# Hub blocks of the second attention layer moved into the drain, the gap and the ramp between two layers

## The chip, the cores and the metric

The kernel runs on one core of a Trainium2 chip. The metric is the device time of one execution in microseconds; times given are the median of several executions. The profile comes from one further execution with the hardware profiler on.

## What is computed

The input is a batch of 8 graphs with the same 2048 nodes and 64 features per node, and one adjacency matrix of 2048 x 2048 zeros and ones. Two layers of graph attention are followed by layer normalisations:

```python
def _gat_layer(h, mask, b):
    scores = jnp.einsum('...nd,...md->...nm', h, h)
    scores = jnp.where(mask, scores, NEG)
    attn = jax.nn.softmax(scores, axis=-1)
    return jnp.einsum('...nm,...md->...nd', attn, h) + b

mask = graph + jnp.eye(N, dtype=graph.dtype) > 0
h = jnp.einsum('bnc,hdc->bhnd', x, Wh)              # 4 heads
out_h = _gat_layer(h, mask[None, None], bh[None, :, None, :])
cat = jnp.transpose(out_h, (0, 2, 1, 3)).reshape(B, N, H * D)
z = jax.nn.leaky_relu(cat, negative_slope=0.2)
h2 = jnp.einsum('bnk,dk->bnd', z, Wo)
out2 = _gat_layer(h2, mask[None], bo)               # 1 head
z2 = jax.nn.leaky_relu(out2, negative_slope=0.2)
out = layernorm(z2) * gamma + beta
result = layernorm(x + out)
```

The adjacency is sparse: node k is linked with a probability that falls with its number, so the first nodes have many neighbours and the later ones few.

## The kernel before

**Tiling.** The first 56 nodes (`HUB`) are "hub" nodes and attend to everything. The other 1992 are put into 166 sets of 12 nodes (`NS`, `SET`). For each set the kernel makes a list of at most 128 nodes that some member of the set is linked to; the attention of the 12 members is then computed densely over the 128 rows of that list, with a mask. The rows are fetched with an indirect DMA, issued by GpSimd (`gather`, one per set and layer: 332 in all). A row has the features of all 8 batches, 2080 bytes. `table1` holds the rows for layer 1, `table2` the rows that layer 1 leaves for layer 2, and `table3` the terms x + beta of the last normalisation; all three lie in DRAM.

**Order of the work.** The order of instructions on each engine is the order in which the program writes them; nothing is moved by a planner. So the source is a software pipeline written out by hand, and each engine (TensorE, VectorE, ScalarE, GpSimd) and each DMA queue (SP, ScalarE, GpSimd) works through its own list in that order, waiting where an operand or a buffer isn't ready.

**Stage 0** (about the first 150 us) reads the adjacency, makes the lists for the first 60 sets (the others follow within layer 1), and does the hub nodes of layer 1.

**Layer 1** is a loop `for i in range(-4, NG + 3)` over 83 groups of two sets (`NG`). Iteration i has, for different groups: `scores` (L821), `weigh` (the mask, VectorE, L826), `project` (L531) and `leaky` into `z` (L518), a copy of the transposed rows (`xTg`, L1030), `lift` (exp, L833), `values` (L846), `invert` (reciprocal L853 and product `osb` L854), the gathers of group i + 5, `leak` (L523), `second_maps` (L880) and `second_rows` (L890), `columns` (L806), `keep_own` (L885) and `keep_rows` (L894, and the stores of `rowt` to `table2`, L897), `keep_columns` (the copy `y`, L812), and the transposes of the gathered rows (`turn`, L512) and of the values (L863, copied to `otb`, L870). PSUM is divided in four tiles of two banks with the tags T (transposed rows), S (scores), C (`cat`: projections, maps, rows, columns) and O (values), one buffer each. The iterations i = 83 to 85 are the drain: the last groups pass through the later steps.

**The gap.** Then the pools of stage 0 and layer 1 are closed and those of layer 2 opened (`late`, `psum2`). VectorE clears the buffers of layer 2 (`ownb` L1107, `bd` L1111, `esh` L1113, `es2` L1114 and L1115) and makes the mask `linked` (L1117). The first 24 gathers from `table2` are issued, and four loads of hub rows (L1267).

**Layer 2** is a loop `for u in range(-4, NU + 7)` over 42 groups of four sets (`NU`); u = -4 to -1 is the ramp. Iteration u has `scores2` of u + 2 (L1133, exp at L1136), `values2` of u (L1165), the four gathers of u + 6, `spread_own` (L1124), `turn_scores` (L1144) and `keep_scores` (L1152) of u + 1, and `turn2` of u + 4 (transposes L512, copies `xTg` L1320). The gathered rows have 24 buffers, six groups. The hub nodes attend to all nodes in 18 blocks (17 of ten sets, and the hub itself); `hub_at` says in which iterations they are done: u = -4 to -1 and then every second one from 2 to 28. A block has a load of rows by SP (`hub_block`), `hub_scores2` (L1277), `hub_lift2` (VectorE L1285, exp at L1288) and, two iterations later, `hub_values2` (L1299), which adds into `oh2`.

**Norms.** After each second group the sums of eight sets are normalised (`norm`, lines L1186 to L1222), in eight steps spread over eight iterations: division, leak, mean, centring, sum of squares, root (`roots`, on ScalarE, L1239 and L1240), then gamma, the row of `table3`, and a second normalisation; `store` (L1248) writes eight pieces of 24 KB to the output, issued by SP. Only the last norm issues half of its pieces from ScalarE.

At the end the kernel reads a flag that says whether the lists were long enough; if they weren't, `general_kernel` would compute everything again. With these inputs it doesn't run.

## Time and profile before

| | us |
|---|---|
| median of 3 runs (lowest, highest) | 877.46 (876.76, 881.76) |
| profiled execution | 880.76 |
| its span | 878.9 |
| busy: TensorE, its weight loads, VectorE, ScalarE, GpSimd | 753.0, 661.2, 610.1, 514.4, 469.2 |
| layer 1's last values (L846) begin | 590.42 |
| first gather of layer 2 begins | 605.49 |
| last gather of layer 2 begins | 822.80 |
| the last group of `values2` (L1165) begins | 846.38 |
| VectorE's last instruction ends | 869.43 |

Times within the kernel are counted from the start of the span. The profile names engines PE (TensorE's matmuls), PEld (its weight loads), DVE (VectorE), ACT (ScalarE), POOL (GpSimd) and SP (the SyncE queue, which only issues DMAs here); a q behind a name is the engine's instruction queue, where DMAs are issued. L512 is line 512 of the kernel before. A group is named by line, engine, operation and "written tile <- read tiles". "x16" counts instructions. In a timeline, the bracket gives the idle time before an instruction and what ended it, as inferred from semaphores. The chain of waits is followed back from the last instruction, at each step to what released it; there the times of matmuls are those between their ends. All times of pieces come from the one profiled execution.

### The profile page before, as it was taken

What the parts mean: (1) busy time and instruction counts of PE and PEld (TensorE: products, weight loads), DVE (VectorE), ACT (ScalarE), POOL (GpSimd) and SP (SyncE); (2) the same over time, 40 slices, a digit from 0 to 9 for tenths busy, and PEclk for the clock granted to TensorE, in tenths of its full rate; (3) what the DMA queues carried; (4) which work ended last, traced back from release to release, by engine and by line L of the source; (5) the groups of instructions that cost most, each with busy time, mean ns of one, the idle gap of its engine ahead of it and who ended that gap; (6) DMA issues with size and microseconds to landing.
All of it is one profiled execution on the core that took longest, in us unless ns stands there. A gap on an engine that the chain in (4) does not pass through costs nothing.

```text
span 878.9 us, 42066 instructions
## 1 busy us (share of the span) xinstructions
PE 753.0 (86%) x18437; PEld 661.2 (75%) x18437; DVE 610.1 (69%) x1369; ACT 514.4 (59%) x961; POOL 469.2 (53%) x612
## 2 busy tenths in 40 slices
PE   1896777889999999999999999992999999998730
PEld 1664456778788999988999999971899999988720
DVE  3356983568888788877555555553258999998994
ACT  2342333556556667666766667651678888886821
POOL 5654141457444555655666666503777777777300
PEclk9998998999999999999999999995999999999965
DMA  8787451355434445655566665514888888888611
GB/s 167 238 218 213 129 146 48 83 142 160 109 100 118 112 125 159 162 169 153 160 168 173 160 166 162 134 28 114 246 266 253 275 275 267 266 252 242 172 46 35
DMA packets 81794, 145.22 MB, mean 165 GB/s; under 512 B 30146, under 2 KB 46466, under 8 KB 81602
## 3 DMA queue, kind: packets, MB, share of 16 engines
q0 software_dynamic: 26720, 88.55, 36.4%
q1 hardware_dynamic: 37842, 49.65, 18.7%
q10 hardware_dynamic: 17040, 4.25, 2.6%
q8 instruction: 147, 2.41, 1.1%
q14 instruction: 45, 0.37, 0.1%
HBM read 123.91 MB, written 18.48 MB: 162 GB/s over the span
## 4 chain that ended last, share of the span: by engine, by line
PE 63%; DVE 15%; DMA 7%; ACT 5%; issue 4%; SPq 3%; POOL 2%; DVEq 0%; ACTq 0%; POOLq 0%
PE t L512 11%; PE s L821 10%; PE o L846 10%; PE cat L806 6%; PE o L863 4%; PE cat L531 4%; PE cat L880 3%; PE s L1133 3%; PE o L1165 3%; PE cat L890 2%; DMA raw<-in_adj_dram 2%; SPq L1248 2%; PE sh L1277 2%; PE e L1144 2%; DMA g<-table,index 1%
## 5 line engine op out<-in xcount | busy, mean ns | idle before, releaser
L792 POOL DMA_INDIRECT g<-table,index x332 | 334.9, 1009 | 236.1 <-PE o L846 140.2
L512 PE MATMUL t<-ident,g 128*128 128x128 f32 x1328 | 182.3, 276 | 15.6 <-DMA g<-table,index 12.7
L512 PEld LDWEIGHTS t<-ident,g 128*128 128x128 f32 x1328 | 154.8, 142 | 20.0 <-issue 14.0
L826 DVE TENSOR_TENSOR e<-s,mask 128x768 f32<-128x768 f32 x83 | 79.4, 956 | 87.4 <-PE s L821 85.4
L518 ACT ACTIVATE z<-cat,bhp 128x192 f32<-128x192 f32 x166 | 60.8, 418 | 85.0 <-PE cat L531 85.0
L846 PE MATMUL o<-g,e 128*64 128x65 f32 x2656 | 97.5, 227 | 0.0
L821 PEld LDWEIGHTS s<-y,xTg 64*64 64x64 f32 x5312 | 85.2, 134 | 13.9 <-issue 13.7
L821 PE MATMUL s<-y,xTg 64*64 64x48 f32 x5312 | 95.5, 220 | 0.0
L846 PEld LDWEIGHTS o<-g,e 128*64 128x64 f32 x2656 | 85.8, 140 | 9.8
L1320 ACT COPY xTg<-t 128x1024 f32<-128x1024 f32 x83 | 80.3, 1017 | 18.1 <-PE t L512 17.3
L1030 ACT COPY xTg<-t 128x1024 f32<-128x1024 f32 x83 | 84.0, 1012 | 2.0 <-PE t L512 2.0
L833 ACT ACTIVATE e<-e,shifts 128x768 f32<-128x768 f32 x83 | 79.2, 955 | 2.1 <-DVE e L826 1.7
L812 ACT COPY y<-cat 128x384 f32<-128x384 f32 (+1 forms) x80 | 40.7, 508 | 64.0 <-PE o L863 40.1
L597 ACT ACTIVATE e<-e,shifts 128x896 f32<-128x896 f32 x32 | 33.4, 1042 | 73.0 <-DVE e L594 52.1
L680 POOL TENSOR_SCALAR a<-raw 120x1024 bf16<-120x1024 int32 (+1 forms) x34 | 38.2, 1125 | 65.1 <-DMA raw<-in_adj_dram 38.4
L806 PE MATMUL cat<-xo,gram 128*128 128x192 f32 (+1 forms) x320 | 65.6, 328 | 0.0
L853 DVE RECIPROCAL rall<-o 64x8 f32<-64x8 f32 x166 | 34.0, 205 | 42.0 <-PE o L846 40.7
L854 DVE TENSOR_TENSOR osb<-o,rall 128x512 f32<-128x512 f32 x83 | 57.4, 692 | 2.9
L1165 PE MATMUL o<-g,es 128*32 128x65 f32 x2656 | 49.1, 226 | 5.9 <-DVE y_s L1188 4.5
L806 PEld LDWEIGHTS cat<-xo,gram 128*128 128x128 f32 x320 | 53.7, 203 | 0.3 <-issue 0.2
L1165 PEld LDWEIGHTS o<-g,es 128*32 128x32 f32 x2656 | 46.1, 113 | 7.0 <-issue 4.9
L1133 PE MATMUL s<-xTg,bd 128*32 128x128 f32 x1328 | 45.4, 277 | 6.2 <-ACT bd L1124 3.5
(177 smaller groups left out, 1369.3 us busy)
## 6 DMA issues: line engine op xcount, KB each, us to landing
raw<-in_adj_dram SPq DMA_DIRECT2D x32, 480.0 KB
table<-xb SPq DMA_DIRECT2D x22, 256.0 KB
xr_s<-table SPq DMA_DIRECT2D x21, 256.0 KB
g<-table,index POOLq DMA_INDIRECT x332
table<-x SPq DMA_DIRECT2D x16, 260.0 KB
x<-in_x_dram ACTq DMA_DIRECT2D x32, 128.0 KB
table<-rowt SPq DMA_DIRECT2D x166, 24.4 KB
xb<-in_x_dram SPq DMA_DIRECT2D x164, 24.0 KB
```

The source lines that it names most:

```text
L512: nc.tensor.transpose(tp[:, q * P:(q + 1) * P], rows[:, q, 1:1 + P], ident)
L518: nc.scalar.activation(z[:, hp], cat[:, :, hp * n:(hp + 1) * n], AF.Identity, bias=bhp[:, hp:hp + 1], scale=1.0)
L792: nc.gpsimd.indirect_dma_start(out=t.rearrange("n q c -> n (q c)"), out_offset=None, in_=table, in_offset=bass.IndirectOffsetOnAxis(ap=ind ...
L806: nc.tensor.matmul(cat[:, k, 2 * GM:2 * GM + n], gram[:, g % 2 * 2 + k, :], held["x", g // 2][:, :n], start=True, stop=True)
L821: nc.tensor.matmul(sp[half(r), p, (q * 2 + j) * M:(q * 2 + j + 1) * M], xt[half(p), j, q, half(r)], y[half(p), (j * Q + q) * M:(j * Q + q ...
L826: nc.vector.tensor_tensor(e[:, :16 * M].rearrange("p (a q n) -> p a q n", a=2, q=Q), sp[:, :, :8 * M].rearrange("p a (q n) -> p a q n", q= ...
L833: nc.scalar.activation(e[:, :16 * M], e[:, :16 * M], AF.Exp, bias=shifts[:, 0:1], scale=1.0)
L846: nc.tensor.matmul(op[half(p), j, o0:o0 + K1], e[:, c0:c0 + 64], rw[j][:, q, sums(p)], start=True, stop=True)
L1030: nc.scalar.copy(t, held.pop(("tp", i + 2)))
L1133: nc.tensor.matmul(sp[q * 32:(q + 1) * 32, k, :], bd[u % 3][:, k, q, :], xt[:, s % 2, q, :], start=True, stop=True, tile_position=(0, q * 32))
L1165: nc.tensor.matmul(op[t * 32:(t + 1) * 32, f, k * W2 + p:k * W2 + p + K1], e[:, 2 * q + p, k, :], rw[:, q, sums(p)], start=(a == 0 and k = ...
L1320: nc.scalar.copy(t, tp)
```

## The change

1. *Shared buffers.* A list `share` of six buffers in the pool that lives through the kernel replaces buffers of stage 0 (`wnat`, `wos`, `number`, `yh`, `keys`, `cand`, `best`) and later serves layer 2 (`ownb`, `bd`, `es2`, `esh`). `linked` takes a part of `maskh` that is no longer needed.
2. *Early clearing.* Eleven jobs (clearing `ownb` and copying into it, five clearings of `bd` and `es2`, ends, `linked`, three `spread_own`) are done one at a time in the odd iterations 61 to 81 of layer 1.
3. *Hub steps.* `hub_step(k)` does scores and lift of block k and the values of block k - 1. Steps 0 to 5 run in iterations 80 to 85 of layer 1, steps 6 to 10 in the gap, 11 to 14 in the ramp and 15 to 18 in u = 0 to 3. The order of blocks begins with the hub itself. The rows of the first ten blocks are loaded in iterations 78 to 82 into buffers of layer 1's gathered rows, the next four in the gap. Scores and sums of the hub use the two banks of a PSUM tile `both`, which also takes the place of layer 1's T, of layer 2's scores and of `oh2`.
4. *Drain.* Iteration 84 uses the tag S for `cat` instead of C, and the last two groups issue one of their two stores to `table2` from ScalarE.
5. *Last norms.* The last four set norms are done in three steps over three iterations instead of eight; in three of them the products with gamma and the sums with the row of `table3` go to GpSimd. The hub's norm starts at u = 4. The last norm's eight stores are issued from SP, ScalarE and GpSimd in turn.

The core of the diff:

```diff
+    share = [const.tile([P, n], F32, name=f"share{k}") for k, n in enumerate([HALFN, HALFN, HALFN, 512, 512, 2 * 456])]
...
-            nc.sync.dma_start(out=dst[2 * g + j], in_=r[j * 48:(j + 1) * 48])
+            (nc.scalar if j and g >= NG - 2 else nc.sync).dma_start(out=dst[2 * g + j], in_=r[j * 48:(j + 1) * 48])
...
+    both = psumk.tile([P, 2, 512], F32, name="both")
...
-        return psum1.tile([P, 2, 512], F32, tag=tag, name=name)
+        return both if tag == "T" else psum1.tile([P, 2, 512], F32, tag=tag, name=name)
...
+    def clear_own():
+        nc.vector.memset(ownb, 0.0)
+        for p in range(2):
+            nc.vector.tensor_copy(ownb[half(p), :, p, :], ownh[half(p)].rearrange("c t (k n) -> c (t k) n", k=2))
+    def clear_ends():
+        for k in range(2):
+            nc.vector.memset(esh[k][:, Q * 2 * HUB:], 1.0)
+        nc.vector.memset(es2[0][:, :, :, 24:], 1.0)
+    def link():
+        nc.vector.tensor_scalar(linked, mask.rearrange("p s (k h) -> p s k h", h=H)[:, :, :, 0], 0.0, None, OP.is_equal)
...
+    hub_order = [NHB] + list(range(NHB))
+    oh2 = both[:, 1, :]
...
+    def hub_step(k, sp):
+        if k <= NHB:
+            hub_scores2(k, sp)
+            hub_lift2(k)
+        if 0 < k <= NHB + 1:
+            hub_values2(k - 1)
+    ahead_of_second = ([clear_own] + [lambda t=t: nc.vector.memset(t, 0.0) for t in bd + es2] + [clear_ends, link] +
+                       [lambda u=u: spread_own(u) for u in range(3)])
...
-        cat = one(f"cat{i}", "C")
+        cat = one(f"cat{i}", "C") if i <= NG else None
+        if i < NG:
+            ph, pr = cat[:, 0, 384:384 + GM], cat[:GM, 1, 384:512]
+        else:
+            cat = one(f"cat{i}", "S" if i == NG + 1 else "C")
+            ph, pr = cat[:, 0, :GM], cat[:GM, 1, :P]
...
+        if NG - LOOK <= i < NG:
+            for j in range(2):
+                k = 2 * (i - NG + LOOK) + j
+                hub_block(k, rows_tile(f"gh{k}"))
...
+        if i >= 60 and i % 2 and ahead_of_second:
+            ahead_of_second.pop(0)()
         if 0 <= (i - 30) // 2 <= NV:
             (add_beta if i % 2 else load_own)((i - 30) // 2)
         if 0 <= i - 1 < NG:
             leak(held["z", i - 1])
...
+        if i >= NG - 3:
+            hub_step(i - NG + 3, both[:, 0, :])
+    for k in range(6, 11):
+        hub_step(k, both[:, 0, :])
...
+    xts = [late.tile([P, 2, 512], F32, name=f"xts{k}", bufs=1) for k in range(6)]
+    hrows = [late.tile([P, Q, PW], F32, name=f"hrows{k}", bufs=1) for k in range(4)]
+    for k in range(4):
+        hub_block(10 + k, hrows[k])
     for u in range(6):
         for s in sets[u]:
             gather(table2, s, 2, rows2)
...
-        at = [v + 2, v + 6]
+        quick = 2 * NV - 7 <= v < 2 * NV and nb == 8
+        at = [v + 1, v + 2] if quick else [v + 2, v + 6]
...
         def again():
             scale(0)
-            nc.vector.tensor_tensor(y, y, row(gam), OP.mult)
-            nc.vector.tensor_tensor(y, y, xr[:, :nb], OP.add)
+            eng = nc.gpsimd if quick and v < 2 * NV - 1 else nc.vector
+            eng.tensor_tensor(y, y, row(gam), OP.mult)
+            eng.tensor_tensor(y, y, xr[:, :nb], OP.add)
...
+        if quick:
+            return [([], [first, act, mean(0), centre(0)]), ([var(0)], [again, mean(1), centre(1)]), ([var(1)], [end])]
...
-                    (nc.scalar if v == NV - 1 and a else nc.sync).dma_start(out=dst, in_=y[p0:p0 + SET].rearrange("p (f w) c -> p f (w c)", f=2)[:, :, :w * D])
+                    queue = nc.sync if v < NV - 1 else (nc.sync, nc.scalar, nc.gpsimd)[(2 * t + a) % 3]
+                    queue.dma_start(out=dst, in_=y[p0:p0 + SET].rearrange("p (f w) c -> p f (w c)", f=2)[:, :, :w * D])
...
-        if u - 2 in hub_at:
-            b = hub_at[u - 2]
-            hub_values2(b, b == 0, b == NHB)
...
+        k = u + 15
+        if k <= NHB + 1:
+            hub_step(k, bank2(f"sh{k}", "T", 2)[:, 0, :] if k <= NHB else None)
+            if 10 <= k - 1 and k + 3 <= NHB:
+                hub_block(k + 3, hrows[(k - 1 - 10) % 4])
+        if u == 4:
+            spread(u, norm_hub(u, oh2))
```

## The prediction, written before the changed kernel was run

> **What bounds the kernel now.** I read the busy table by slices first (TensorE at 9 tenths almost everywhere, so the ends of the stages matter), then windows over each stage, then the chain of waits inside the second layer, then the timeline of the gap, of one late iteration of layer 1 and of the end. The windows give, per stage: span, busy PE, PEld, DVE, ACT, POOL, granted clock, DMA share.
>
> ```profile
> 558.50:578.50 20.00, 20.00 (x557) 18.15 (x553) 11.74 (x30) 13.66 (x29) 7.40 (x11) 1.00 0.38 95
> 590.00:600.00 10.00, 6.84 (x96) 5.04 (x96) 3.39 (x11) 2.00 (x6) 0.80 (x3) 0.70 0.06 14
> 700.00:720.00 20.00, 19.77 (x508) 18.34 (x507) 18.31 (x34) 16.19 (x30) 15.26 (x16) 1.00 0.89 276
> 820.00:840.00 20.00, 15.47 (x468) 13.74 (x456) 19.45 (x36) 14.65 (x29) 2.98 (x3) 1.00 0.44 125
> ```
>
> The end of layer 1's loop is pure TensorE (20.00 of 20). The drain (590 to 600) is half idle at a reduced clock. Layer 2 has TensorE at 19.77, but VectorE at 18.31 and DMA at 0.89 stand close behind. After 820 VectorE is the bound. The chain of waits through one pair of layer-2 iterations (start, us, what):
>
> ```profile
> 708.75 1.02 ACT xTg L1320
> 709.78 0.04 issue
> 709.82 1.09 PE sh L1277 x8
> ...
> 713.46 1.75 PE t L512 x16
> ...
> 717.15 0.62 PE oh L1299 x16
> 717.77 0.59 PE e L1144 x4
> 718.36 0.89 PE t L512 x8
> ```
>
> The pair lasts 719.27 - 708.75 = 10.52 us. The hub block costs 0.62 (oh) and, because its scores need a transposing bank, 0.89 + 1.06 + 1.09 where the other iteration has only 1.75: 1.29 more. So 1.91 us per block; without it TensorE needs 8.6 us per pair. But GpSimd's gathers (a pair has 8) have a pace of their own, seen where no buffer holds them:
>
> ```profile
> 606.76 0.95 POOL L792 DMA_INDIRECT g<-table,index  x1 [0.30 <-issue]
> 608.01 0.95 POOL L792 DMA_INDIRECT g<-table,index  x1 [0.30 <-issue]
> ...
> 610.29 1.20 DVE L1117 TENSOR_SCALAR linked<-mask 128x1992 uint8<-128x1992 uint8 x1
> 610.51 1.79 POOL L792 DMA_INDIRECT g<-table,index  x1 [0.30 <-issue]
> ```
>
> One every 1.25 us: 10.0 us per pair. **The floor under layer 2 is therefore the gather queue, 0.5 us below the present pair, not TensorE's 8.6.** The third view is one late iteration of layer 1:
>
> ```profile
> 559.56 0.55 DVE L523 SCALAR_TENSOR_TENSOR z<-z 128x384 f32<-128x384 f32 x1
> 560.19 0.28 DVE L894 TENSOR_TENSOR rowt<-cat,bob 96x128 f32<-96x128 f32 x1
> 560.56 0.51 ACT L812 COPY y<-cat 128x384 f32<-128x384 f32 x1 [0.66 <-PE o L863]
> 560.95 0.54 ACT L870 COPY otb<-o 128x192 f32<-128x192 f32 x2
> 561.79 0.38 PEld L531 LDWEIGHTS cat<-otb,whT 64*64 64x64 f32 x16
> ```
>
> ScalarE's y copy starts 0.09 us after VectorE's rowt in every iteration looked at; otb ends at 561.49 and TensorE's projection begins at 561.79. What delays rowt has about 0.28 us of slack before TensorE stops.
>
> **What the skill says.** "DMA: Bandwidth & Descriptors", section SWDGE vs HWDGE vs iDMA: descriptors of a GpSimd DMA are built by GpSimd's cores in software. The 0.95 us per gather agrees. "SBUF — State Buffer", Who interferes with whom: VectorE and GpSimd share a port pair, and some VectorE forms shut out GpSimd's descriptor writing. The 1.79 us gather beside the 1.20 us linked instruction agrees. "PSUM — Partial Sum Buffer", PSUM bank collisions raise a hardware error: accesses of one bank by two engines have to be kept apart. The 0.09 us agrees with an order kept between VectorE and ScalarE on cat. "TensorE: Matmul & The Clock Gate", Part 1: an idle window takes the clock to half. The 32 values matmuls that take 1.15 us in the loop take 1.88 at 590.42.
>
> **The change part by part.**
>
> 1. *Clearing in the loop.* Eleven jobs go into odd iterations 61 to 81, on VectorE between osb and leak, so ahead of rowt. Their durations are in the gap's timeline: ownb memset and two copies 1.03, three bd memsets 1.57 together, two es memsets 0.91 each plus 0.1 between, ends about 0.45, linked 1.20: 6.2 us in eight VectorE jobs. Less 8 x 0.28 slack: **+3.8 us** on a saturated TensorE (bounds: 0 if y didn't wait for rowt, 5). The three spreads (two copies, 0.70) fit ScalarE's 0.66 us of idle before y: 0. In the gap all of this but the 0.43 ownb memset was hidden beside gathers in flight, so little comes back there.
>
> 2. *Hub blocks in the drain.* Steps 0 to 5 follow the value transposes of iterations 80 to 85. Each has scores (1.03), VectorE lift 0.62, ScalarE exp 0.66, values 0.62. Iteration 80 is saturated: +1.03. From 81 on, values 0.62 join; some of it fills the 0.67 us waits for otb at 589.93 and 595.03, and the clock stays up (0.73 back on the values at 590.42). Followed in order: values 82 end 593.3 instead of 592.3, projection 82 starts 596.6 instead of 595.03, second maps 82 600.6 instead of 597.95, last rowt 603.3 instead of 600.40. The S bank for iteration 84 is in this already: maps 82 no longer wait for rowt 80. The two last stores are issued from SP and ScalarE side by side (0.58 each, now in a row, the last at 601.43) and land 2.04 later: 606.3 instead of 604.1. **+2.2 us** (0 to 4). Ten hub loads of 244 KB take the place of layer-1 gathers on an idle DMA (share 0.05); SP issues each in 0.77 and in those five iterations has 2 x 0.77 + 2 x 0.6 = 2.7 of 4.8 us: 0. First gather of layer 2, in before's clock: 605.5 + 3.8 + 2.2 = 611.5. GpSimd's 0.9 us of queued waits after the last landing stay.
>
> 3. *Gap and ramp.* Steps 6 to 10 run on TensorE at about 1.7 us each while the gathers fly; the first set was usable 5.6 us after its issue. Four hub loads stand ahead of the gathers as four did before: even. Steps 11 to 14 answer to the four blocks that the ramp had; 15 to 18 run in iterations 0 to 3.
>
> 4. *Layer 2.* First to last gather now takes 822.80 - 605.49 = 217.3 us for 165 intervals; at 1.25 it is 206.3. Iterations 0 to 3 with a hub step need about 4.3 + 1.9 = 6.2 us against 5.0. The 24 buffers give set group 6 at 30 us after the first gather; TensorE frees group 0 about 27.5 us after it. After four such iterations it is 1.1 us late, and that remains. 1 us for stray waits: 208.4. VectorE: 19.3 busy of two pairs now, 9.65 per pair, less lift 0.62 = 9.0: under 10.0. **-8.9 us** (bounds -11 and 0, the last if VectorE takes over). The hub's own norm moves to iterations 4 to 11, where the set norms still build up: 0.
>
> 5. *Last norms.* From the gap after iteration 35 VectorE is the bound. Two of 13 instructions in each of three norms go to GpSimd: 0.73 x 2 saved, but the mean stands directly behind them in VectorE's queue and waits for both; at 1.28 each (GpSimd's add of bet, same shape) that is about 2.75: +1.3 net x 3 = +3.9. Gone are the remains of the hub norm (0.8) and some idle. VectorE's work from iteration 36 to its end sums to 47 us against 44.3. In exchange TensorE, ahead of the gathers rather than behind, ends values 35 some 4 us before the last group's gathers are issued (0.9 before now). Sum **-0.8 us** (-5 to +3).
>
> 6. *Stores.* After VectorE's last instruction (869.43) SP still has eight stores of norm 19 and four of norm 20 to issue, until 874.95 (5.5 us). Norm 19 now ends 10 us earlier; norm 20's eight go out on three queues, about 1.6 us on SP and 2 on GpSimd, whose landing is slower. **-3.2 us** (-1 to -4).
>
> Sum: +3.8 + 2.2 - 8.9 - 0.8 - 3.2 = -6.9. The profiled execution took 880.76 us (span 878.9 and 1.9 around it), so 873.9; the median of the runs is 877.46, 3.3 under the profiled one, so I forecast **870.6 us**.
>
> **Rivals.**
> - *The clearing is free and the quick norms pay.* If rowt's delay is absorbed (-3.8) and GpSimd's two steps overlap other VectorE jobs (-3.9): 863. For it: the y copy's named releaser is PE o, not rowt, in most iterations. Against: the same 0.09 us everywhere, also where PE o had ended 0.26 earlier.
> - *The gathers wait for the hub steps.* If the memory of the gathered rows is shared with that of the hub rows in the closing pool, the first gather comes only after step 10: 603.3 + 3.8 + 6 x 1.7 + 0.6 = 617.9, and the 1.3 us of waits and issue give 619.2, 7.7 later: 878.3. For it: the page's first gather waits for something of VectorE's after the landing. Against: the tiles opened ahead of the rows look sized to keep them on older memory.
> - *Slower: VectorE takes TensorE's place in layer 2.* Decides from 5.26 us per iteration without hub work. Then layer 2 gives nothing (-8.9 lost) and the end stays behind VectorE by its 47 us (+3): 870.6 + 8.9 + 3 = 882.5. For it: 18.31 of 20 us busy, 19.45 after 820. Against: there, without hub blocks, iterations of 4.96 to 4.99 us were reached.
>
> **How the numbers follow.** Forecast case 0.50, free clearing 0.27, waiting gathers 0.12, VectorE 0.11. A measurement of this kernel can hardly tell less than 1% (8.8 us) from no change; the bounds are 868.7 and 886.2. Of the forecast's 0.50, with parts 1 to 6 varying, 0.14 lies under 868.7; with most of the second case faster makes 0.40. Slower than 886.2: the upper part of the last case and the forecast's extremes, 0.09. Range 862 to 882: below it a part of the second case, above it half of the last.
>
> **What would show it.** Right: odd layer-1 iterations from 61 on at 5.2 to 5.9 us, with TensorE waiting for otb; first layer-2 gather near 611; its gathers at 1.25 us without a break after iteration 4; layer-2 TensorE with idle ended by gather landings; VectorE idle of 2 to 3 us beside GpSimd in the last three set norms; SP silent 2 us after VectorE ends. Wrong: odd iterations still 5.0; gathers held up by TensorE or VectorE at 5.2 us or more per iteration; the first gather after the hub steps.

## The result and the profile after

The changed kernel takes **913.6 us** (median of 4, 911.01 to 917.09) against 878.0 for the kernel before: ratio 1.0385, 95% interval 1.0348 to 1.0422. I had forecast 870.6 with a range to 882. The profiled execution has a span of 914.2 us, 35.3 more than 878.9. Cut at the same events in both profiles, the 35.3 us lie here:

| stretch | before | after | difference | my sum |
|---|---|---|---|---|
| start to first weigh of layer 1 | 153.4 | 157.7 | +4.3 | 0 |
| first to last weigh | 432.7 | 438.0 | +5.3 | +4.8 |
| last weigh to last rowt | 14.4 | 18.5 | +4.1 | +1.9 |
| last rowt to first gather of layer 2 | 5.1 | 16.2 | **+11.1** | -0.7 |
| first to last gather | 217.3 | 225.8 | **+8.5** | -8.9 |
| last gather to VectorE's last instruction | 46.6 | 52.0 | **+5.4** | -0.8 |
| from there to the end of the span | 9.5 | 6.1 | -3.4 | -3.2 |

(The +1.03 for the first hub scores, which I had in the sum of the drain, falls into the second row; the third row's +1.9 and the fourth's -0.7 are 603.3 for 600.40 and 2.2 in all, less that 1.03.)

The windows of the changed kernel over the end of the layer-1 loop, the drain, the stream of layer 2 and its tail (span, busy PE, PEld, DVE, ACT, POOL, granted clock, DMA share, GB/s):

```profile
568.00:588.00 20.00, 19.36 (x547) 17.52 (x546) 12.02 (x29) 13.67 (x30) 6.78 (x10) 1.00 0.42 112
600.00:610.00 10.00, 6.92 (x134) 5.77 (x134) 4.31 (x12) 3.34 (x8) 0.54 (x2) 1.00 0.31 90
725.00:745.00 20.00, 17.96 (x468) 16.34 (x466) 18.50 (x34) 16.73 (x30) 15.73 (x15) 1.00 0.84 239
856.00:876.00 20.00, 12.05 (x292) 10.71 (x285) 14.36 (x24) 10.19 (x24) 3.63 (x4) 0.83 0.28 76
```

As forecast, the drain's clock stays at 1.00 and TensorE is less busy in layer 2 (17.96 instead of 19.77 of 20). But GpSimd is no faster for it, and in the tail VectorE, which should have been the bound, is busy for only 14.36 of 20 us. The gap of the kernel before, from its last rowt to its first gather (start, us, engine, line, idle before and who ended it):

```profile
600.40 0.29 DVE L894 TENSOR_TENSOR rowt<-cat,bob 96x128 f32<-96x128 f32 x1 [0.61 <-PE cat L890]
605.05 0.43 DVE L1107 MEMSET ownb<- 128x448 f32 x1 [4.36 <-DMA table<-rowt]
605.49 0.96 POOL L792 DMA_INDIRECT g<-table,index  x1 [5.56 <-DVE ownb L1107]
605.51 0.57 DVE L1109 COPY ownb<-ownh 64x224 f32<-64x224 f32 x2
```

The same stretch of the changed kernel:

```profile
614.09 0.29 DVE L895 TENSOR_TENSOR rowt<-cat,bob 96x128 f32<-96x128 f32 x1 [1.07 <-DMA table<-rowt]
...
620.08 0.62 DVE L1074 TENSOR_TENSOR share<-both,maskt 120x448 f32<-120x448 f32 x1 [1.92 <-PE both L1065]
620.80 0.69 PE L1088 MATMUL both<-gh,share 120*64 120x65 f32 x16 [0.83 <-issue]
621.42 1.09 PE L1065 MATMUL both<-share,own 128*120 128x112 f32 x8
622.62 0.62 DVE L1074 TENSOR_TENSOR share<-both,maskt 120x448 f32<-120x448 f32 x1 [1.92 <-PE both L1065]
...
628.77 0.69 PE L1088 MATMUL both<-gh,share 120*64 120x65 f32 x16 [1.19 <-issue]
629.60 3.21 SPq L1054 DMA_DIRECT2D hrows<-table  x4
630.29 0.97 POOL L793 DMA_INDIRECT g<-table,index  x1 [18.07 <-PE both L1088]
```

Before, the first gather comes 5.1 us after the last rowt, once the table's last store has landed. Here the last rowt is at 614.09, yet the first gather starts at 630.29, right behind the values of hub step 10 (628.77), which it names as releaser. And a step takes 2.54 us (620.08 to 622.62), not 1.7: scores, lift and values follow one another, with TensorE idle for 0.83 us ahead of each values. The end of the last norm, where the stores now stand on three queues:

```profile
907.41 0.69 DVE L1299 TENSOR_TENSOR y_s<-y_s,var_True 128x512 f32<-128x512 f32 x1 [0.61 <-ACT var_True L1328]
908.13 1.35 SPq L1337 DMA_DIRECT2D out_dram<-y_s  x3
908.14 1.24 ACTq L1337 DMA_DIRECT2D out_dram<-y_s  x3
908.40 1.28 POOL L1337 DMA_DIRECT2D out_dram<-y_s  x2 [16.43 <-DVE y_s L1299]
```

All are issued within 1.6 us of VectorE's end. This step is as forecast.

One thing is needed to read the runs below: in three of their five sets the kernel before itself took 1,041 to 1,048 us (median), and in every kernel profiled there layer 2's gathers took 297 to 324 us from first to last, with GpSimd waiting for row buffers; from these sets ("slowed transfers") I read the gap, layer 1's loop, the length of single gathers and the tail, and differences of whole times only where I say so.

### The profile page after: what moved, and what is told of

The parts are those of the page before. It is cut to its first block, busy times and chain, and to the rows that moved or that the text cites. A ratio compares the mean times of both kernels' runs of the same rounds, so it can differ in the third digit from the quotient of the medians.

```text
span 914.2 us, 42292 instructions
## 1 busy us (share of the span) xinstructions
PE 765.4 (84%) x18437; PEld 666.5 (73%) x18437; DVE 609.6 (67%) x1363; ACT 519.2 (57%) x969; POOL 485.5 (53%) x620
## 4 chain that ended last, share of the span: by engine, by line
PE 58%; DVE 16%; DMA 10%; ACT 6%; issue 5%; POOL 3%; SPq 2%; ACTq 0%; DVEq 0%; POOLq 0%
PE s L822 9%; PE o L847 9%; PE both L513 8%; PE cat L807 5%; DMA g<-table,index 4%; PE cat L532 4%; PE o L864 3%; DMA raw<-in_adj_dram 3%; PE cat L881 3%; PE t L513 2%; PE cat L891 2%; PE both L1216 2%; DMA table<-x 2%; DVE st_s L1279 2%; PE oh L609 1%
## 5 line engine op out<-in xcount | busy, mean ns | idle before, releaser
L793 POOL DMA_INDIRECT g<-table,index x332 | 342.5, 1032 | 252.8 <-PE o L847 139.2
L513 PE MATMUL both<-ident,g 128*128 128x128 f32 x664 | 100.7, 275 | 2.7 <-DVE share L709 2.5
L513 PE MATMUL t<-ident,g 128*128 128x128 f32 x664 | 87.8, 282 | 17.0 <-DMA g<-table,index 14.6
L1369 ACT COPY xts<-t 128x1024 f32<-128x1024 f32 x83 | 81.1, 1016 | 30.2 <-PE t L513 21.6
L513 PEld LDWEIGHTS t<-ident,g 128*128 128x128 f32 x664 | 76.1, 145 | 22.6 <-DMA g<-table,index 12.8
L1123 ACT COPY xTg<-both 128x1024 f32<-128x1024 f32 x83 | 84.0, 1012 | 1.7 <-PE both L513 1.7
L513 PEld LDWEIGHTS both<-ident,g 128*128 128x128 f32 x664 | 80.1, 142 | 5.8 <-DVE share L709 3.1
L1286 ACT ACTIVATE sq_s<-y_s 128x512 f32<-128x512 f32 x42 | 26.4, 629 | 47.9 <-DVE y_s L1284 47.8
```

The source lines that it names most:

```text
L513: nc.tensor.transpose(tp[:, q * P:(q + 1) * P], rows[:, q, 1:1 + P], ident)
L793: nc.gpsimd.indirect_dma_start(out=t.rearrange("n q c -> n (q c)"), out_offset=None, in_=table, in_offset=bass.IndirectOffsetOnAxis(ap=ind ...
L1123: nc.scalar.copy(t, held.pop(("tp", i + 2)))
L1369: nc.scalar.copy(t, tp)
```

## The experiments

A set is a group of runs made together on one chip. Whole times are compared within a set, beside the runs of the kernel before that it shares; pieces of time come from one profile of each run, and where they are compared across sets the text says so.

### What holds the gathers in the gap

First run (the changed kernel with steps 6 to 9 out of the gap; its hub norm, moved to u = 9, shares a variance buffer with a set norm, which leaves output rows of both wrong):

```diff
...
-                hub_block(k, rows_tile(f"gh{k}"))
+                if k < 6:
+                    hub_block(k, rows_tile(f"gh{k}"))
...
-    for k in range(6, 11):
-        hub_step(k, both[:, 0, :])
+    hub_values2(5)
...
-        hub_block(10 + k, hrows[k])
+        hub_block(6 + k, hrows[k])
...
-        k = u + 15
+        k = u + 10
...
-        if u == 4:
+        if u == 9:
```

> The changed kernel with hub steps 6 to 9 taken out of the gap: only blocks 0 to 5 use the gathered rows' buffers of layer 1, blocks 6 to 9 load into the late hub rows and are worked off in the first iterations of layer 2, four iterations later everything. Theory 'memory': the gathers waited because their rows lie on the memory that hub blocks 0 to 9 used, so with the last such reader (block 5) at the end of the drain the first gather comes about 5 us after the last rowt, near 619.5 instead of 630.3, and the kernel takes 8 to 11 us less than the changed kernel, about 903 to 906. Rival 'order': the gathers wait for something else of the gap (the loads' queue, the table's last stores with the clock), then the first gather stays within 3 us of 630 and the time stays at 910 to 916. If the stream of layer 2 pays for the four steps moved into it (0.6 of GpSimd's row buffers held longer, VectorE 0.62 per step), the gain is 5 to 8.

Second run (the steps of the gap get other banks for their scores):

```diff
     for k in range(6, 11):
-        hub_step(k, both[:, 0, :])
+        hub_step(k, one(f"shs{k}", "SCO"[k % 3])[:, 0, :])
```

> The changed kernel with the scores of hub steps 6 to 10 in the three score, column and value banks that the drain has left free, instead of one bank of the pair whose other bank holds the hub sums. Theory 'pair': values k-1 wait for lift k because both banks belong to one pair, so the wait of 0.83 us per step goes and a step takes about 1.7 us: the first gather comes 4 us earlier (near 626) and the kernel takes 3 to 4.5 us less than the changed one. Rival 'weights': the wait comes from the two halves of the hub weights lying in one buffer; then the steps stay at 2.5 us and the time does not move.

Measured in a set with slowed transfers: 1,035.4 and 1,028.3 us; the kernel before 1,045.6. Last rowt to first gather is 3.8 us in the first run and 11.35 in the second; in the seven profiles with the gap of the changed kernel it is 16.2 to 19.3. In these nine and in the two profiles of the combined run below, the first gather starts 0.84 or 0.85 us after the end of the last values that read the layer-1 row buffers, wherever the edit puts them. (In the second run its bracket names VectorE's lift, which had ended 0.38 us before; in the changed kernel that distance is 1.62.) So the first gather follows the last reader of these buffers: "memory" is shown, "order" falls. Neither run has the changed kernel in its set, so the 8 to 11 us and the 3 to 4.5 us expected of the whole time are not tested. In the timeline of the second run the steps look so:

```profile
644.77 0.62 DVE L1074 TENSOR_TENSOR share<-shs,maskt 120x448 f32<-120x448 f32 x1 [1.01 <-PE shs L1065]
645.21 1.09 PE L1065 MATMUL shs<-share,own 128*120 128x112 f32 x8
646.23 0.69 PE L1088 MATMUL both<-gh,share 120*64 120x65 f32 x16
646.41 0.62 DVE L1074 TENSOR_TENSOR share<-shs,maskt 120x448 f32<-120x448 f32 x1 [1.01 <-PE shs L1065]
...
651.04 0.96 POOL L793 DMA_INDIRECT g<-table,index  x1 [13.22 <-DVE share L1074]
```

1.64 us per step (644.77 to 646.41), and TensorE goes from scores to values without a pause. So "pair" holds: as long as the scores lay in one bank of `both` and the hub sums in the other, values waited for VectorE's lift of the next block. The two halves of the hub weights still lie in one buffer here, so "weights" falls.

### What sets the pace of layer 2

The kernel before without the hub blocks of its steady state, three times (the hub rows of the output are incomplete):

```diff
-    hub_at = {u: b for b, u in enumerate([-4, -3, -2, -1] + list(range(2, 2 * NHB, 2))[:NHB - 3])}
+    hub_at = {u: b for b, u in enumerate([-4, -3, -2, -1])}
...
```

> The kernel before with hub blocks 4 to 17 left out of the second layer (loads, scores, lift and values; the hub rows of the output are then incomplete), the hub's norm at its old place. It prices what the change takes out of the steady state of layer 2. My prediction's theory: the gathers then run at 1.25 us, first to last gather 206 to 209 us instead of 217.3, the kernel at about 869. Rival 'stretch': GpSimd was the bound already, [...]so the blocks cost nearly nothing there: 214 to 217 us, and the kernel stays within 4 us of the kernel before.

> The kernel before with hub blocks 4 to 17 left out of the second layer, as in the run of that kind above, whose transfers were slow. My prediction's theory: gathers at 1.25 us, first to last gather 206 to 209 us instead of 217.3, the kernel about 9 us below the kernel before. Rival 'stretch': GpSimd was the bound already, held up beside VectorE's two-input instructions, and the stream takes 213 to 217 us, the kernel within 4 us of the kernel before.

> Once more the kernel before with hub blocks 4 to 17 left out of layer 2 (incomplete hub rows), beside a kernel before whose transfers are not slowed, if this set has one. My prediction's theory: 206 to 209 us from first to last gather instead of 217.3. Rival 'stretch': 213 to 217 us, as the gathers' own durations summed to 10 us over 0.95 each in the kernel before and fell to 0.95 each once the norms were left out.

The first two fell into sets with slowed transfers (998.6 and 999.6 us beside 1,045.6 and 1,048.1). The third did not: **886.5 us against 880.3**, ratio 1.0072 (1.0047 to 1.0096), and its first to last gather takes 219.2 us, no less than the 217.3 with the hub blocks. Fourteen blocks at 1.9 us of TensorE each bring nothing. That it is even 0.7% slower I can't explain; its profiled execution, the fastest of 16, has the span of the kernel before. In both kernels GpSimd never waits longer than 0.31 us between two gathers of this stretch: it is saturated. A piece of the kernel before:

```profile
705.35 0.69 DVE L1197 TENSOR_REDUCE st_s<-y_s 128x8 f32<-128x512 f32 x1
705.54 0.94 POOL L792 DMA_INDIRECT g<-table,index  x1 [0.30 <-issue]
706.55 0.69 DVE L1202 SCALAR_TENSOR_TENSOR y_s<-st_s,y_s 128x512 f32<-128x512 f32 x1
706.79 1.27 POOL L792 DMA_INDIRECT g<-table,index  x1 [0.30 <-PE o L1165]
```

And of the kernel without the hub blocks:

```profile
703.61 0.68 DVE L1202 SCALAR_TENSOR_TENSOR y_s<-st_s,y_s 128x512 f32<-128x512 f32 x1
703.76 1.35 POOL L792 DMA_INDIRECT g<-table,index  x1 [0.30 <-issue]
705.42 0.94 POOL L792 DMA_INDIRECT g<-table,index  x1 [0.31 <-issue]
706.67 0.95 POOL L792 DMA_INDIRECT g<-table,index  x1 [0.30 <-PE t L512]
```

Some gathers take 1.27 or 1.35 us instead of 0.95. Next, also without the hub blocks, the first 17 set norms are cut:

```diff
+        if i < 17:
+            return [([], [first]), ([lambda: store(y)], [])]
         return [([], [first, act, mean(0)]), ([centre(0)], []), ([var(0)], []), ([], [again, mean(1)]), ([centre(1)], []),
...
```

> The same, and of the first 17 set norms of layer 2 only the division and the store are kept, with all loads and stores (the rest of these norms is left out, so their output rows are not normalised). Theory 'stretch': without VectorE's two-input instructions the gathers take 0.95 us and 0.30 between them, 206 to 209 us from first to last. Rival 'transfers': the DMA engines, at 0.89 before, set the pace, and the stream stays at 213 to 217 us.

> The kernel before without hub blocks 4 to 17 in layer 2 and with the first 17 set norms cut to division and store (that output is not normalised), beside a kernel before whose transfers are not slowed. Theory 'stretch': the gathers take 0.95 us each again and come every 1.25 us, first to last 207 to 209 us instead of 219.2 with the norms, and the kernel about 10 us under the run without hub blocks. Rival 'transfers': the DMA engines set the pace, 217 to 219.

In the undisturbed set: **868.4 us against 880.5**, ratio 0.9878 (0.9829 to 0.9927), first to last gather 207.6 us, within the forecast 207 to 209. In the other set (991.0 beside 1,048.1) the stream was hardly shorter (297.2 for 299.2), but the gathers' own durations fell from 166.7 to 157.8 us in sum, 0.95 each; here from 169.9 to 158.3. The timeline:

```profile
701.75 0.95 POOL L792 DMA_INDIRECT g<-table,index  x1 [0.30 <-issue]
703.00 0.94 POOL L792 DMA_INDIRECT g<-table,index  x1 [0.30 <-issue]
704.25 0.95 POOL L792 DMA_INDIRECT g<-table,index  x1 [0.30 <-issue]
```

"Stretch" is shown: the norms, not TensorE and not the DMA engines, add 10 to 12 us to the stream. The cut also takes the norms' squares and roots off ScalarE, so which instructions it was has to come from the traces. They leave little doubt. A norm on VectorE has seven steps whose two inputs both lie in SBUF: leak, two centrings, two scalings, the product with gamma, the sum with the input row. In the kernel before, 60 of layer 2's 166 gathers start while such a step runs; 49 of them take over 1.00 us, up to 1.45. Of the others only the one beside `linked` does (1.79); the remaining 105 take at most 0.96 us, also those that start during a VectorE step that reads PSUM or has a single input. The excess of each of the 49 is the rest of the step that was running, less 0.13 us, to within 0.02 us: above, the centring that runs from 706.55 to 707.24 has 0.45 us left when the gather starts at 706.79, and the gather takes 0.95 + 0.32 = 1.27. The 52 long gathers without hub blocks and the 50 of the changed kernel follow the same line. The 49 are spread over all these kinds of step. The other 11 of the 60 have 0.14 us or less of the step left or start within 0.02 us of it.

### The closed-up norms

The changed kernel with the norms wholly on VectorE (three times), and with the old norms:

```diff
-            eng = nc.gpsimd if quick and v < 2 * NV - 1 else nc.vector
+            eng = nc.vector
```

```diff
-        quick = 2 * NV - 7 <= v < 2 * NV and nb == 8
+        quick = False
```

> The changed kernel with the two steps of the last norms (times gamma, plus input) back on VectorE, all else kept. Theory: each of three norms loses 2.7 us of VectorE's wait for GpSimd and gets 2 x 0.73 of work back, so the time from the last gather to VectorE's last instruction falls from 52.0 to 48.2 us and the kernel takes 3 to 4.5 us less. Rival: TensorE's iterations (6.8 to 10 us at the end) hang on other links, and the tail stays within 1.5 us of 52.

> The changed kernel with the last norms closed up but wholly on VectorE, beside a kernel before whose transfers are not slowed. With GpSimd's steps worth 4 us and the closing up 5 (the old norms gave a tail of 43.2 for 52.0, but 3.6 us more of stores behind it), the tail is 47 to 49 us and the kernel takes 3 to 4.5 us less than the changed kernel's 913, about 909. If the GpSimd steps are hidden, 913.

> The changed kernel with the closed-up norms wholly on VectorE, once more, now beside the changed kernel on one chip. The profile gave a tail shorter by 4.8 us (47.2 for 52.0), the time no difference that could be told. Theory: the 4 to 5 us are in the time as well, so this run is 3 to 5 us below the changed kernel beside it. Rival: the tail is counted from the last gather, and a later last gather or a lower clock takes it back: within 1.5 us of the changed kernel.

> The changed kernel with the last norms as in the kernel before (spread over eight iterations, all on VectorE), all else kept. Theory: closing the norms up is what lengthened the tail, by GpSimd's steps and by VectorE standing for ScalarE's squares and roots; with the old norms the last gather to VectorE's end takes 46 to 48 us instead of 52. Rival: closing up is worth about 4 us by itself and only GpSimd's steps cost (the run with them on VectorE won 4 us of tail); then the tail stays at 51 to 54 us.

| kernel | last gather to last values | last values to VectorE's end | VectorE busy, of both together |
|---|---|---|---|
| before | 24.7 | 22.0 | 42.8 of 46.6 |
| changed | 33.3 | 18.7 | 36.0 of 52.0 |
| changed, norms closed up on VectorE | 29.7 | 17.5 | 39.6 of 47.2 |
| changed, old norms | 21.0 | 22.2 | 38.7 of 43.2 |

Each row is one profile; the changed kernel's, the one on VectorE and the one with old norms are from three sets. Without GpSimd's steps the tail is 4.8 us shorter here, and 4.0 with slowed transfers (58.2 to 54.2 within one set, and the same two figures between two others). The time doesn't show it: 912.8 us in a set beside 880.5, where the changed kernel had 913.6 beside 878.0; 1,028.6 beside the changed kernel's 1,029.5; and 1,034.0 beside 1,045.6 in the third run, which has no changed kernel in its set. In the first of these profiles the drain fell to a clock of 0.57 for 7 us and the gap took 38.9 us instead of 34.7; so I can't say that the 4 us are lost, nor that they are won. With old norms the tail is 8.8 us shorter and the time 912.8 (beside 880.3), since the end behind VectorE is 9.7 us instead of 6.1 and the stream 2.4 longer.

How the closing up lengthens the way to the last values is in the timeline of the changed kernel's tail:

```profile
860.84 0.68 DVE L1299 TENSOR_TENSOR y_s<-y_s,var_True 128x512 f32<-128x512 f32 x1
861.60 1.26 POOL L1304 TENSOR_TENSOR y_s<-y_s,gam 128x512 f32<-128x512 f32 x1 [4.53 <-DVE y_s L1299]
862.95 1.26 POOL L1305 TENSOR_TENSOR y_s<-y_s,xr_s 128x512 f32<-128x512 f32 x1
864.24 0.69 DVE L1279 TENSOR_REDUCE st_s<-y_s 128x8 f32<-128x512 f32 x1 [2.72 <-POOL y_s L1305]
864.96 0.69 DVE L1284 SCALAR_TENSOR_TENSOR y_s<-st_s,y_s 128x512 f32<-128x512 f32 x1
...
865.69 0.63 ACT L1286 ACTIVATE sq_s<-y_s 128x512 f32<-128x512 f32 x1 [5.36 <-DVE y_s L1284]
866.22 0.67 ACT L1219 ACTIVATE eT<-both,shifts 128x512 f32<-128x512 f32 x1
...
866.95 1.12 PE L1227 MATMUL both<-ident,eT 128*128 128x128 f32 x4 [5.79 <-ACT eT L1219]
```

VectorE waits 2.72 us for GpSimd; ScalarE's square waits 5.36 us for VectorE's centring; behind the square, in ScalarE's queue, stands the exponential of the next scores (866.22), though these were ready at 860.24; and TensorE waits 5.79 us for that. Three engines stand for one step. With the norms closed up wholly on VectorE the same exponential still starts 4.6 us after its scores (868.62 for 864.06), with the old norms 0.1 us after them (862.97 for 862.90). Slower matmuls have a part in the longer way, which was not separated: from the last gather to the last values the granted clock is 0.91 before, 0.74 in the changed kernel, 0.83 with the norms closed up on VectorE and 0.92 with the old norms.

### All three undone, and the clearing behind rowt

```diff
-        if i >= 60 and i % 2 and ahead_of_second:
-            ahead_of_second.pop(0)()
         if 0 <= (i - 30) // 2 <= NV:
...
             turn(tp[:, 1, :], rows[1, 2 * (i + 3) + 1])
+        if i >= 60 and i % 2 and ahead_of_second:
+            ahead_of_second.pop(0)()
         if i >= NG - 3:
```

with the first edit of the gap (here with the hub norm at u = 10) and the norms on VectorE. It was run twice.

> The changed kernel with three parts undone at once: hub steps 6 to 9 out of the gap and behind the gathers (hub norm at iteration 10), the last norms wholly on VectorE, and the clearing jobs at the end of their iteration, behind rowt, instead of ahead of it. By the sums so far: gap -11 to -12, tail -4, loop -3 to -4, so about 19 us under the changed kernel, 894 to 897. If rowt has no part in the cost of the clearing, the loop keeps its 438.0 us (first to last weigh) and 3 to 4 us are missing.

> The changed kernel with hub steps 6 to 9 behind the gathers, the last norms wholly on VectorE and the clearing behind rowt, as in the run above that had slowed transfers. Sums: gap 22 to 24 instead of 34.7, tail 48 instead of 52, loop 434 instead of 438: 892 to 897 where the changed kernel has 912 to 914. The stream keeps 222 to 228 us, since GpSimd's pace isn't TensorE's. If the gathers, earlier by 12 us, only wait the longer for row buffers that the moved hub steps hold, the stream grows by as much and the time stays near 905.

The first run fell into a set with slowed transfers: 1,026.8 us, where the changed kernel beside it took 1,039.1. The second: 899.0 us beside 880.5, ratio 1.0219 (1.0171 to 1.0268); the changed kernel had 1.0385. That is 2 us above the range that I expected. The loop takes 432.5 us, what it took before the change, and 460.1 against the changed kernel's 464.4 and 461.8 in sets with slowed transfers. So the clearing is free where nothing waits behind it, though its first copy is held up there too (1.41 us for 0.28), and rowt was what carried its price. The gathers start 3.8 us after the last rowt:

```profile
606.14 0.29 DVE L895 TENSOR_TENSOR rowt<-cat,bob 96x128 f32<-96x128 f32 x1 [1.07 <-PE cat L891]
607.74 1.23 PEld L1088 LDWEIGHTS both<-gh,share 120*64 120x64 f32 x32 [0.98 <-issue]
609.25 3.22 SPq L1054 DMA_DIRECT2D hrows<-table  x4
609.95 0.96 POOL L793 DMA_INDIRECT g<-table,index  x1 [6.44 <-PE both L1088]
```

But the stream grew to 231.3 us. GpSimd's waits for TensorE's values from 610 to 720 us (us in all, number, longest):

```profile
POOL g L793 <- PE o L1246: 16.4, 13, 3.9
```

GpSimd waits for row buffers there: 12.8 us beyond the usual 0.30 between gathers over the whole stream (5.1 in the changed kernel, none in the kernel before). With a hub step in each of u = -4 to 8 TensorE is the slower one again, so 5.5 us of the 12 that this kernel wins between the last rowt and the first gather were given back in the stream.

### The changed kernel again

> The changed kernel itself, once more, as the measure for runs of this set and to see how much stage 0 (first weigh of layer 1 at 157.65 us, 4.3 later than in the kernel before) varies by itself. If the shared buffers cost those 4.3 us, the first weigh comes 3 to 5 us later than in the kernel before again; if it was the variation of a run, it may come anywhere from 153 to 158.

> The changed kernel itself, as the measure for the run beside it, with five rounds: 911 to 916 us where the kernel before has 878 to 881, last rowt to first gather 16.2 us as in each run of it so far, tail about 52 us.

1,039.1 and 1,029.5 us, beside 1,048.1 and 1,040.6: where transfers are slowed, the changed kernel is 1.0 to 1.2% faster than the kernel before. I have no profile of the kernel before there, so why stays open; that its hub blocks cost it something there is seen from the runs without them (ratio 0.956 and 0.955). The first weigh came at 165.9 and 157.8 us here; in the undisturbed sets it came at 155.1, 152.6 and 158.2 in kernels with shared buffers and at 151.8 to 156.1 in those without. The 4.3 us of stage 0 are therefore within what varies from run to run; a cost of the shared buffers of 2 us or less would not be seen.

### Two versions of the kernel before

Two small parts of the change alone (columns in bank S and ScalarE's queue at the end of layer 1, three store queues), then the same with GpSimd's help in the norms that end after the last gather:

```diff
-            nc.sync.dma_start(out=dst[2 * g + j], in_=r[j * 48:(j + 1) * 48])
+            (nc.scalar if j and g >= NG - 2 else nc.sync).dma_start(out=dst[2 * g + j], in_=r[j * 48:(j + 1) * 48])
...
-        cat = one(f"cat{i}", "C")
+        cat = one(f"cat{i}", "S" if i == NG + 1 else "C")
...
-                    (nc.scalar if v == NV - 1 and a else nc.sync).dma_start(out=dst, in_=y[p0:p0 + SET].rearrange("p (f w) c -> p f (w c)", f=2)[:, :, :w * D])
+                    queue = nc.sync if v < NV - 1 else (nc.sync, nc.scalar, nc.gpsimd)[(2 * t + a) % 3]
+                    queue.dma_start(out=dst, in_=y[p0:p0 + SET].rearrange("p (f w) c -> p f (w c)", f=2)[:, :, :w * D])
```

> The kernel before with two small parts of the change alone: the last norm's eight stores on three queues, and at the end of layer 1 the last columns in the score bank with the second of the last stores on ScalarE's queue. My prediction's sums: stores -3.2 us (VectorE's last instruction to the end of the span 6.1 instead of 9.5), drain -1 to -2 (last weigh to first gather of layer 2 near 18 instead of 19.5), so 4 to 5 us under the kernel before. Rival: the last stores of a norm before them, still on one queue, end as late, and only 1 to 2 us are won.

```diff
+        apart = 2 * NV - 10 < v < 2 * NV - 1 and nb == 8
...
+            eng = nc.gpsimd if apart else nc.vector
-            nc.vector.tensor_tensor(y, y, row(gam), OP.mult)
-            nc.vector.tensor_tensor(y, y, xr[:, :nb], OP.add)
+            eng.tensor_tensor(y, y, row(gam), OP.mult)
+            eng.tensor_tensor(y, y, xr[:, :nb], OP.add)
...
+        if apart:
+            return [([], [first, act, mean(0)]), ([centre(0)], []), ([var(0)], []), ([], [again]), ([], [mean(1), centre(1)]),
+                    ([], []), ([var(1)], []), ([end], [])]
```

> The kernel before with the two small parts (three store queues, columns in the score bank and ScalarE's queue at the end of layer 1), and in the set norms 16 to 19, whose steps come after the last gather, times gamma and plus input on GpSimd, with the mean that follows them moved half an iteration and more back, beside the centring, so that VectorE has other work meanwhile. Theory: after the last gather VectorE is the bound and 4 x 2 x 0.71 us leave it, so tail 46.1 less 4 to 5.7 us, about 872 to 874 where the kernel before has 880. Rival: GpSimd's steps slow VectorE's beside them, or VectorE runs out of other work, and the tail stays within 2 us of 46.

The first takes **878.2 us against 880.3** (ratio 0.9971, 0.9953 to 0.9989): the one complete version that is faster than both kernels, by 0.3% or 2.1 us, for the 4 to 5 that I expected. Its last weigh to first gather is 17.4 instead of 19.5; behind VectorE's end it wins only 0.5 us (8.9 for 9.5), as the rival said: the norm before still has eight stores in SP's queue. The three queues are worth 3.4 us only where that norm ends early. The second can't be told from the kernel before (881.1 beside 880.5, ratio 0.9994, 0.9974 to 1.0015): VectorE's busy time in the tail falls from 42.2 to 37.0 us, and the tail is 47.4 instead of 46.1. VectorE stands idle for TensorE (2.0 and 2.3 us) and for GpSimd (1.58 twice).

## Why the prediction was wrong

Against my sums, step 4 is off by 17.4 us, step 3 by 11.8, step 5 by 6.2, the drain by 2.2, and stage 0 came 4.3 later. Either of the first two alone turns a gain of 6.9 us into a loss.

**What held.** Part 1 in its mechanism: the clearing ahead of rowt makes iterations longer, and the run with the clearing behind rowt gives them back. Its size was near by luck. From the weigh of group 60 to the last, the loop takes 117.1 us instead of 109.5, and 0.9 of these 7.6 lie in the last interval, with the first hub scores; so the clearing cost about 6.7 us, more than the forecast 3.8 (6.2 less 8 x 0.28 is 4.0) and than its bound of 5. The +5.3 of the whole loop hides it because the iterations up to there happened to be 2.3 us shorter in this profile. And 4.1 us came from the first job alone, which I had not priced so. The iteration with it in the changed kernel's layer 1:

```profile
491.16 0.43 DVE L1032 MEMSET share<- 128x448 f32 x1
491.62 2.14 DVE L1034 COPY share<-ownh 64x224 f32<-64x224 f32 x2
492.34 1.28 POOL L929 TENSOR_TENSOR xb<-xb,bet 128x512 f32<-128x512 f32 x1
494.44 0.28 DVE L895 TENSOR_TENSOR rowt<-cat,bob 96x128 f32<-96x128 f32 x1
494.81 0.50 ACT L813 COPY y<-cat 128x384 f32<-128x384 f32 x1 [3.43 <-DVE rowt L895]
495.79 0.56 PE L532 MATMUL cat<-otb,whT 64*64 64x96 f32 x16 [2.31 <-ACT otb L871]
```

The two copies took 2.14 us beside GpSimd's addition of bet, where the gap of the kernel before has 0.57: a duration taken from a place where GpSimd did something else. The first took its usual 0.27; the second began at 491.91, while a gather ran, and ended 0.15 us after the addition. The Trainium skill's page "SBUF — State Buffer", section Who interferes with whom, has copies among the forms that can contend with GpSimd for the shared port pair, with the engine that comes second blocked for the whole instruction of the other; the trace agrees. Part 6 held as well (-3.4 for -3.2), as long as the norm before the last ends early. The first rival's free clearing fell.

**Step 3 failed by its overlap.** I wrote that steps 6 to 10 run "while the gathers fly". They don't, because the gathers' buffers lie on the memory that those steps read. I had this as a rival (0.12) and set it low on a guess about how the memory is laid out; the trace of the kernel before couldn't tell, for there the gap had no reader of those buffers in it. I also priced it too low, at 7.7 us from 1.7 per step, where a step takes 2.54: I had not asked what lies in the other bank of the pair that the scores use. Last rowt to first gather alone cost 11.1 us, and the gap all in all (with the drain, mis-sized by 2.2) 15.2 instead of 1.2; with readers and banks moved, the first gather came 3.8 us after the last rowt and a step took 1.64.

**Step 4 failed by its floor.** I took 1.25 us per gather, the pace where VectorE is quiet, as the pace that the gathers would reach once TensorE let them, and read the gathers' mean of 1.32 us as TensorE's doing. The gathers of the kernel before already stood 0.30 us apart throughout; it was their own durations (168.0 us in sum, for 157.8 to 158.3 without norms) that made up the difference. The section of the Trainium skill's page "SBUF — State Buffer" that I had cited for one instruction in the gap, Who interferes with whom, also says that a VectorE instruction with two inputs from SBUF contends with a GpSimd instruction that reads SBUF. A set norm has seven such steps, and a gather reads its indices from SBUF. The runs agree and give the price here, 10 to 12 us over 166 gathers, and the traces show when it is paid: when a gather starts while such a step runs, and then for the rest of that step. So the forecast gain of 8.9 us was not to be had from TensorE's work: without fourteen hub blocks the stream took 219.2 us. My rival with VectorE as the bound of layer 2 (0.11) came nearest, but VectorE sets the pace by holding up gathers, not by its own busy time. On top, the steps moved into u = 0 to 3 gave row buffers back late: 5.1 us of waits, for the 1.1 that I had written. The other 3.3 of the 8.5 us are longer gathers, 171.3 us in sum for 168.0.

**Step 5 failed by a queue that I left out.** GpSimd's cost was right in size in the profiles (+3.9 forecast, 4.0 to 4.8 in the tails), though the times don't show it, and so was the gain when TensorE isn't behind (21.0 instead of 24.7 with old norms). But closing up by itself costs 8.7 us on the way to the last values (29.7 for 21.0), where centring's square stands ahead of the next scores' exponential in ScalarE's queue and the clock is lower; the share of each is open. I had looked only at who is behind the waiting instruction on VectorE. The gains behind the last values are real, 4.7 us up to VectorE's end (17.5 for 22.2) and 3.7 in the stores after it (6.0 for 9.7), but they only make up for it: both runs took 912.8 us, in sets with 880.5 and 880.3 for the kernel before.

## What to carry to other kernels

Before an engine is relieved, look at the idle time between the instructions of the others: one whose idle time is constant and minimal is already the bound, and if its instructions vary in length, find what was running when the long ones started. Work put into a gap between two stages has to be followed to the buffers it reads and the banks it shares, for what starts after the gap may wait on exactly these. Where a chain of short steps is closed up across engines, list what stands behind each waiting instruction on every engine it passes.

## What the runs showed of the hardware

- An indirect gather of 128 rows keeps GpSimd for 0.95 us, with 0.30 to the next. One that starts while VectorE runs a step with two inputs from SBUF takes longer by the rest of that step less 0.13 us (49 of 49 long gathers of the kernel before, `linked` apart), and a stream of 166 takes 217 to 219 us instead of 207.6.
- Two VectorE copies of 64x224 took 2.14 us beside a gather and a GpSimd addition of 128x512, for 0.57 us in the gap of the kernel before.
- With hub work in the drain the clock stayed at 1.00 in one profile and fell to 0.57 over 7 us in another of the same code there, where 8 matmuls took 1.78 us instead of 0.99.
- The same change made the kernel 3.9% slower where transfers ran freely and 1.0 to 1.2% faster where they were slowed.
